# Spreading layer 0 unevenly over the chunks of a state-space scan

## Chip, cores and metric

The kernel runs on one core of a Trainium2 chip. The metric is device time in microseconds (us), from the launch to the end of the core's work; lower is better. Besides the timed runs there is one profiled execution, from which every duration below is taken.

## What is computed

Thirty-two images of 128 channels and 56 x 56 pixels, all float32, go through four layers. Each layer first normalises its input over groups of four channels, and adds its result to the input:

- Layer 0: a 128 x 128 mix of the channels, whose weights depend on the image, and then three depthwise 3 x 3 convolutions of the result with dilations 1, 3 and 5, each through SiLU and added up.
- Layer 1: a fixed cubic spline of each value.
- Layer 2: a linear attention with eight heads, then a depthwise 3 x 3 convolution.
- Layer 3: a Mamba block. Its core is a recurrence over the 3136 pixels of an image, for 256 inner channels with 16 states each.

```python
# layer 0, inside reference(); _gn is the group norm
y = jnp.einsum('boi,bihw->bohw', agg_w, x) + agg_b[:, :, None, None]
for dil in (1, 3, 5):
    c = conv(y, ds_weight, rhs_dilation=(dil, dil), feature_group_count=C)
    out = out + jax.nn.silu(c + ds_bias[None, :, None, None])
...
# layer 3, per token
h = dA_t * h + dBu_t
y = jnp.einsum('bdn,bn->bd', h, C_t)
```

## The kernel before

**Tiling.** An image lies in SBUF as 128 partitions (channels) by 3136 columns, and is worked on in seven chunks of 448 columns (`NCH` = 7). The recurrence of layer 3 treats one chunk in 16 steps (`STEPS`); a step holds two of the 32 pairs of states and channel halves. So an image has 112 steps. In each step VectorE (DVE) multiplies `du` by the rows `pb` (one 128 x 896 multiply, written to `h`) and runs two 448-column scans over `h`; ScalarE (ACT) makes the two decay factors `da`; GpSimd (POOL) multiplies `h` by the rows `cb` into `hc`; TensorE (PE) makes the rows `pb` and `cb`, once in two steps, and adds up `hc` into `y`. Once in a chunk `ssm_inputs` prepares the next chunk on all engines.

**Three images at once.** While the scan of image b runs through its 112 steps, layers 1 and 2 of image b+1 (`until_scan`, called `rest`) and layer 0 of image b+2 (`first_layer`, called `layer0`) are worked on beside it. The function `images` (L1196) lists all this. The steady loop holds six images a pass, runs five passes, and is followed by the last two images; for those no layer 0 is left. A prologue does layer 0 of two images and layers 1 and 2 of one.

**What paces the work beside the scan.** `first_layer` and `until_scan` are Python generators. Each piece of work that they record ends with `yield` of a number, a rough weight. `Pieces.step(i)` takes pieces until the weight taken reaches the share due at step i. For `layer0` the share grows evenly: there are 108 steps (six chunks of 16, and 12 of the seventh), and its total weight is 90. At step 12 of the seventh chunk `layer0.finish()` takes what is left. `rest` is spread over the first 92 steps. The weight of `layer0` is made up of these parts (`dynamic_conv`, L668): statistics of the seven chunks 7, the group's 3, the mixing weights 6, the mixing of one chunk 1 (`aggregate`, seven times), some 4 around them, and 63 for the **depthwise convolutions**, 21 of them at 3 each.

A depthwise convolution of layer 0 is: one load of a stack of shifted rows from DRAM (four DMAs issued on SP), 12 matmuls on PE (`mm<-stack,dsT`; the profile counts each as two records, so 24), a tanh on ACT (`t`), a multiply on DVE (`g`), an addition on POOL (`xt<-xt,g`), and now and then statistics on DVE (`st`). The convolution of layer 2 has the same form (`mm<-stack,wpT`, seven an image), and its output is added by DVE.

**The order on each engine.** The generators do not issue instructions themselves. They record each as a `Work` with the step at which it is taken. `Plan.order` then gives every work a due time, from its step and from what depends on it, and `attempt` lists the works by a model of the engines: of those that are ready on an engine it takes the one that can start first, and of equals the one due first. No work that stands more than 12 steps ahead of the first unfinished one is considered. The resulting lists, one for each engine, are fixed in the program; each engine runs its own in order, and waits at semaphores. So the step at which a piece is taken bounds its place from below, and the plan decides where it ends up.

Of the kernel before, what the change touches and what calls it, by code (L numbers as in the profile page):

```python
# [23 lines left out]
NCH = L // CH  # L24
# [2 lines left out]
UNROLL = 6  # L27

PREP = 17.5
REST = 92  # L30

G = 32
# [36 lines left out]
STEPS = NPAIR * DI  # L69
# [293 lines left out]
def tile_conv_stack(ctx: ExitStack, tc: tile.TileContext, out: bass.AP, x: bass.AP, w: dict):  # L363
# [223 lines left out]
    class Stats:  # L587


        def __init__(self, xt, st=None):  # L590
            self.xt, self.done = xt, 0
            self.st = small.tile([P, NCH, 6], F32, tag="st", name="st") if st is None else st
# [399 lines left out]
    def gate(xn):  # L992

        for db in range(DI):
            ps = psum()
            nc.tensor.matmul(
                ps, wzT[:, db * P : (db + 1) * P], xn[:, DCONV - 1 :], start=True, stop=True
            )
            silu(sz[:, db, :], ps)
            yield 0.8  # L1000
# [138 lines left out]
    def first_layer(src, b):  # L1139

        xt = xts[b % 3]
        for j in range(NCH):
            nc.sync.dma_start(xt[:, j * CH : (j + 1) * CH], src[:, j * CH : (j + 1) * CH])
        yield from dynamic_conv(xt, sts[b % 2])

    def until_scan(b):

        xt = xts[b % 3]
        st = yield from spline(xt, sts[b % 2])
        st = yield from linear_attention(xt, st)  # L1150
        norm = carried[b % 2]
        norm_weights(st, *norm)
        yield 5.0
        layer_norm(xt, xns[b * NCH % 3], 0, norm)
        yield 5.0

    def first_inputs(b):
        return ssm_inputs(xts[b % 3], b * NCH, carried[b % 2])
# [6 lines left out]
    class Pieces:  # L1165


        def __init__(self, gen, total=1.0, steps=1):
            self.gen, self.total, self.steps, self.taken = gen, total, steps, 0.0

        def step(self, i):
            while self.gen is not None and self.taken < self.total * (i + 1) / self.steps:
                self.next()

        def next(self):
# [16 lines left out]
    xv = x.rearrange("b c l -> c b l")  # L1192
# [3 lines left out]
    def images(first, count, ahead):  # L1196

        def image(v, b):  # L1200
            return v[:, ds(first + b, 1), :].squeeze(1)

        scans = {}

        def new_last():
            return small.tile([P, STEPS, 2], F32, tag="last", name="last")

        def at(g, what):

            if 0 <= g < count * NCH * STEPS:  # L1210
                getattr(scans[g // STEPS], what)(g % STEPS)

        plan.start(FIRST)

        for b in range(count):
            xt = xts[b % 3]
            steps = (NCH - 1) * STEPS + READY
            more = b + 1 < count or ahead
            rest = Pieces(until_scan(b + 1) if more else None, totals[1], REST)
            layer0 = Pieces(first_layer(image(xv, b + 2), b + 2) if b + 2 < count or ahead else None, totals[0], steps)  # L1220
            for j in range(NCH):
                k = b * NCH + j
                if k == 0:
                    last = new_last()
                    scans[0] = Scan(xt, image(ov, 0), last, 0)
                    for n in range(AHEAD):
                        at(n, "c_rows")
                    for n in range(2):
                        at(n, "b_rows")
                    at(0, "decay")  # L1230
                following = None
                if j + 1 < NCH:
                    following = ssm_inputs(xt, k + 1, carried[b % 2])
                elif more:
                    following = first_inputs(b + 1)
                following = Pieces(following, PREP, READY)
                gates = Pieces(gate(xns[k % 3]), 1.6, DI)
                for n in range(STEPS):
                    g = k * STEPS + n
                    plan.at(g)  # L1240
                    if n == 0 and j == NCH - 1:
                        rest.finish()
                    if n == READY:

                        following.finish()
                        gates.finish()
                        if j == NCH - 1:
                            layer0.finish()
                        if k + 1 < count * NCH:
                            nb, nj = divmod(k + 1, NCH)  # L1250
                            if nj == 0:
                                last = new_last()
                            scans[k + 1] = Scan(xts[nb % 3], image(ov, nb), last, k + 1)
                    plan.at(g, FIRST)
                    at(g + 2, "b_rows")
                    at(g, "state")
                    at(g + 1, "decay")
                    at(g, "products")
                    at(g + AHEAD, "c_rows")
                    at(g - LAG + 1, "add")  # L1260
                    at(g - LAG, "store")
                    plan.at(g, SECOND)
                    following.step(n)
                    if n >= READY - DI:
                        gates.step(n - READY + DI)
                    plan.at(g)
                    rest.step(j * STEPS + n)
                    if j * STEPS + n > LAG:
                        layer0.step(j * STEPS + n)
        end = count * NCH * STEPS  # L1270
        for g in range(end - LAG + 1, end):
            at(g, "add")
        at(end - 1, "store")
        plan.issue()

    totals = [0.0, 0.0]
# [7 lines left out]
    with tc.For_i(0, B - 2, unroll) as i:  # L1284
        images(i, unroll, True)
    images(B - 2, 2, False)


# [100 lines left out]
```

## Time and profile before

| what | us |
|---|---|
| median of 3 runs (16321.42 to 16344.79) | 16330.96 |
| the profiled execution, launch to end | 16316.11 |
| its span, first to last instruction | 16314.3 |
| start of the first state multiply (end of the prologue) | 436.0 |
| mean time of one of the 30 images of the loop | 499.8 |
| the last two images | 478.7 and 404.6 |

Counting the state multiplies `h<-du,pb` of the trace, 16 to a chunk, splits each image of the loop into its seven chunks. Means over 30 images, in us:

| chunk | first | second | third | fourth | fifth | sixth | seventh |
|---|---|---|---|---|---|---|---|
| length | 63.8 | 70.4 | 70.4 | 73.0 | 70.9 | 80.7 | 70.6 |
| PE busy | 50.1 | 58.7 | 62.9 | 65.2 | 64.8 | 78.1 | 60.4 |
| DVE busy | 60.0 | 63.8 | 62.8 | 63.3 | 66.8 | 67.6 | 62.0 |
| ACT busy | 45.1 | 60.1 | 64.8 | 61.5 | 48.3 | 45.2 | 40.4 |
| POOL busy | 43.3 | 49.1 | 53.4 | 53.7 | 47.0 | 44.2 | 46.3 |

An engine's busy time close to a chunk's length means that the engine has hardly any idle time there. The sum of a row is the engine's work for one image. Since every engine runs its list in order, a chunk is longer than its busiest engine by the waits that no other work covers.

### The profile page before, as it was taken

Reading aid. Unit: us, or ns where it says so; the run is one execution under the profiler, and the core shown is the slowest. Engines: PE = TensorE matmul, PEld = TensorE weight load, DVE = VectorE, ACT = ScalarE, POOL = GpSimd, SP = SyncE. Lnnn points to the kernel's source line nnn. Section 1 sums busy time; section 2 is a strip of 40 time slices with the busy share of each in tenths; the row PEclk is TensorE's granted clock in tenths of the full one; section 3 lists DMA queues with packets and bytes.
Section 4 is the critical chain, followed back from the end, with each engine's and each line's share of the span. In section 5 each row is a group of like instructions: output and inputs, shape, how many; then the busy total and the mean of one; then the engine's idle time right before and its main releaser. Section 6 shows DMA issues by size and latency. Waiting matters only on the chain. (4 is left out here: it accounts for less than half of the span.)

```text
span 16314.3 us, 212520 instructions
## 1 busy us (share of the span) xinstructions
PE 14202.3 (87%) x66400; PEld 4559.9 (28%) x66400; DVE 14306.2 (88%) x17314; ACT 11713.4 (72%) x21127; POOL 10785.0 (66%) x6406
## 2 busy tenths in 40 slices
PE   6888898888898888988888888888888898888887
PEld 2222222222222222222222222222222222222222
DVE  2898988989889898899988888888898898888889
ACT  3777777777677776777776777767777677776675
POOL 2676666666666666667666666666676666766666
PEclk7888998889998898998989988899988899888888
DMA  6344444344443444434444434444344444344421
GB/s 143 93 101 98 98 112 96 89 99 101 106 104 88 100 97 101 109 94 94 101 99 107 102 86 98 99 105 107 91 98 97 100 108 106 85 97 99 101 56 34
DMA packets 986159, 1589.93 MB, mean 97 GB/s; under 512 B 175622, under 2 KB 611209, under 8 KB 984331
## 3 DMA queue, kind: packets, MB, share of 16 engines
q1 hardware_dynamic: 985002, 1576.06, 41.0%
q8 instruction: 538, 8.81, 0.2%
q14 instruction: 619, 5.06, 0.1%
HBM read 785.62 MB, written 173.18 MB: 59 GB/s over the span
## 5 line engine op out<-in xcount | busy, mean ns | idle before, releaser
L338 POOL TENSOR_TENSOR hc<-h,cb 128x896 f32<-128x896 f32 x3584 | 7476.1, 2092 | 4173.5 <-DVE h L338 2178.7
L338 DVE TENSOR_TENSOR_SCAN h<-da,last,h 128x448 f32<-128x448 f32 x6144 | 6772.7, 1135 | 498.2 <-ACT da L338 451.3
L338 ACT ACTIVATE da<-delta,alog 128x448 f32<-128x448 f32 x7168 | 4481.8, 633 | 2635.3 <-DVE h L338 2369.4
L338 PE MATMUL y<-hc,sums 128*64 128x448 f32 x14336 | 3997.9, 638 | 625.6 <-POOL hc L338 617.8
L338 DVE TENSOR_TENSOR h<-du,pb 128x896 f32<-128x896 f32 x3584 | 3788.6, 1072 | 247.5 <-POOL hc L338 118.2
L338 PE MATMUL mm<-stack,dsT 96*32 96x448 f32 (+1 forms) x16128 | 1890.8, 575 | 59.4 <-DMA stack<-padded 16.8
L338 ACT ACTIVATE hats<-stack,bia,scl 128x448 f32<-128x448 f32 x2688 | 1887.6, 754 | 33.9 <-DVE bia L338 31.7
L338 PE MATMUL mm<-xn,winT 128*128 128x448 f32 x3584 | 1703.8, 590 | 39.8 <-ACT cb L338 13.5
L338 PEld LDWEIGHTS y<-hc,sums 128*64 128x64 f32 x14336 | 807.6, 147 | 2412.9 <-POOL hc L338 1436.9
L338 PE MATMUL mm<-hats,wspl 128*32 128x448 f32 x12544 | 1386.1, 563 | 33.3 <-ACT hats L338 30.4
L338 PE MATMUL pb<-dbl,sel 64*128 64x448 f32 x1792 | 918.3, 512 | 421.2 <-DVE h L338 364.3
L338 ACT ACTIVATE hats<-hats,one 128x1344 f32<-128x1344 f32 x896 | 1261.5, 1408 | 0.1
L338 ACT COPY cb<-mm 128x448 f32<-128x448 f32 x1792 | 940.3, 527 | 379.4 <-POOL hc L338 184.0
L338 PE MATMUL mm<-dbl,sel 64*128 64x448 f32 x1792 | 892.3, 502 | 363.5 <-DVE sz L338 63.7
L338 ACT ACTIVATE t<-mm 128x448 f32<-128x448 f32 x1568 | 829.2, 534 | 484.6 <-PE mm L338 480.3
L338 POOL TENSOR_TENSOR xt<-xt,g 128x448 f32<-128x448 f32 x672 | 767.5, 1142 | 524.1 <-DVE g L338 491.1
L338 DVE TENSOR_TENSOR_SCAN h<-da,h 128x448 f32<-128x448 f32 x1024 | 1054.1, 1070 | 28.3 <-ACT da L338 26.3
L338 PEld LDWEIGHTS mm<-xn,winT 128*128 128x128 f32 x3584 | 631.8, 197 | 986.0 <-issue 805.1
L338 DVE SCALAR_TENSOR_TENSOR g<-t,mm 128x448 f32<-128x448 f32 x672 | 407.7, 607 | 443.7 <-ACT t L338 392.8
L338 PEld LDWEIGHTS mm<-stack,dsT 96*32 96x32 f32 (+1 forms) x16128 | 445.2, 112 | 1156.3 <-issue 899.9
L338 PEld LDWEIGHTS mm<-dbl,sel 64*128 64x128 f32 x1792 | 351.2, 198 | 1453.5 <-issue 420.0
L338 PEld LDWEIGHTS pb<-dbl,sel 64*128 64x128 f32 x1792 | 358.6, 200 | 1419.1 <-issue 791.8
(187 smaller groups left out, 16166.2 us busy)
## 6 DMA issues: line engine op xcount, KB each, us to landing
stack<-padded SPq DMA_DIRECT2D x2688, 264.0 KB
stack<-xt SPq DMA_DIRECT2D x3584, 56.0 KB
delta<-delta SPq DMA_DIRECT2D x1792, 112.0 KB
du<-du SPq DMA_DIRECT2D x1792, 112.0 KB
padded<-yc SPq DMA_DIRECT2D x224, 264.0 KB
padded<-yc SPq DMA_DIRECT2D x256, 231.0 KB
xt<-x_dram SPq DMA_DIRECT2D x224, 224.0 KB
out_dram<-xt SPq DMA_DIRECT2D x224, 224.0 KB
```

The costliest lines, as they stand in the source:

```text
L338: call()
```

## The change

`Pieces` takes a list of paces, one for each chunk of the scan, and adds up the paces of the steps to get the share due at each step. `layer0` is given `PACE`; `rest` and the others keep an even pace. With the paces the 90 units of layer 0 fall on the seven chunks as 18.6, 11.4, 14.3, 14.3, 14.3, 0 and 17.1, where they were 13.3 for each of six chunks and 10 for the seventh.

```diff
+PACE = (1.3, 0.8, 1.0, 1.0, 1.0, 0.0, 1.6)
...
-        def __init__(self, gen, total=1.0, steps=1):
-            self.gen, self.total, self.steps, self.taken = gen, total, steps, 0.0
+        def __init__(self, gen, total=1.0, steps=1, pace=(1.0,) * NCH):
+            self.gen, self.taken = gen, 0.0
+            upto = [0.0]
+            for i in range(steps):
+                upto.append(upto[-1] + pace[i // STEPS])
+            self.upto = [total * u / upto[-1] for u in upto[1:]]
 
         def step(self, i):
-            while self.gen is not None and self.taken < self.total * (i + 1) / self.steps:
+            while self.gen is not None and self.taken < self.upto[min(i, len(self.upto) - 1)]:
                 self.next()
...
-            layer0 = Pieces(first_layer(image(xv, b + 2), b + 2) if b + 2 < count or ahead else None, totals[0], steps)
+            layer0 = Pieces(first_layer(image(xv, b + 2), b + 2) if b + 2 < count or ahead else None, totals[0], steps, PACE)
```

Every instruction of the program stays; only the steps at which those of layer 0 are recorded differ, and with them the lists that the plan makes. The number of instructions on each engine, DMAs included, is the same in both programs.

## The prediction

> **What bounds the kernel now.** I read the page's busy shares first:
>
> ```profile
> span 16314.3 us, 212520 instructions
> PE 14202.3 (87%) x66400; PEld 4559.9 (28%) x66400; DVE 14306.2 (88%) x17314; ACT 11713.4 (72%) x21127; POOL 10785.0 (66%) x6406
> ```
>
> TensorE and VectorE are level, and neither is full: an average over stretches with different limits. So next the windows, over the seven chunks of one image (the third of a pass, a typical one; columns as named in the first line, times in us):
>
> ```profile
> core 0: us, PE busy (x) PEld busy (x) DVE busy (x) ACT busy (x) POOL busy (x), PEclk, DMA share, GB/s
> 7430.30:7497.00 66.70, 51.01 (x161) 17.76 (x162) 60.86 (x84) 45.28 (x83) 43.61 (x25) 0.75 0.25 62
> 7497.00:7564.90 67.90, 56.20 (x238) 17.43 (x236) 62.83 (x81) 59.91 (x107) 48.53 (x30) 0.88 0.27 66
> 7564.90:7635.20 70.30, 62.91 (x337) 19.23 (x338) 63.12 (x74) 65.73 (x116) 54.07 (x34) 0.97 0.47 113
> 7635.20:7707.00 71.80, 64.65 (x349) 19.63 (x351) 62.66 (x74) 60.66 (x110) 53.10 (x33) 0.93 0.39 90
> 7707.00:7777.00 70.00, 63.48 (x329) 24.54 (x322) 66.82 (x83) 48.37 (x91) 47.17 (x30) 0.93 0.47 107
> 7777.00:7858.70 81.70, 78.91 (x430) 23.19 (x432) 67.73 (x79) 45.56 (x91) 44.41 (x25) 0.98 0.60 140
> 7858.70:7924.20 65.50, 55.22 (x248) 18.07 (x240) 60.91 (x72) 40.22 (x65) 45.89 (x29) 0.95 0.50 116
> ```
>
> The sixth chunk stands out: 81.70 us, PE busy for 78.91 of them. In the others DVE is the fullest engine, or ACT in the third (65.73 of 70.30). Then the groups of the sixth chunk, DVE first (after the second bar: idle time before the group, and what ended it):
>
> ```profile
> L338 DVE SCALAR_TENSOR_TENSOR g<-t,mm 128x448 f32<-128x448 f32 x5 | 3.1, 610 | 6.1 <-ACT t L338 6.1
> L338 DVE SCALAR_TENSOR_TENSOR xc<-t,mm 128x448 f32<-128x448 f32 x2 | 1.2, 620 | 3.2 <-ACT t L338 3.2
> L338 DVE SCALAR_TENSOR_TENSOR sz<-t,mm 128x448 f32<-128x448 f32 x3 | 1.8, 609 | 2.4 <-ACT t L338 2.4
> L338 PE MATMUL mm<-stack,dsT 96*32 96x448 f32 (+1 forms) x120 | 13.8, 548 | 0.0
> L338 PE MATMUL mm<-stack,wpT 96*32 96x448 f32 x152 | 15.8, 545 | 0.0
> ```
>
> DVE's idle time there is mostly before three multiplies that need a tanh `t`, 11.7 us; and over the whole span the tanh itself waits for the matmul in front of it (480.3 of its 484.6 us idle, `t<-mm` on the page). Five of the waiting ones are `g`, layer 0's own. So here PE is late, DVE stands in its list before `g`, and the scans behind `g` stand with it. Last, finer windows of the same image: steps 24 to 35, then 80-83, 84-87, 88-91, 92-95 and 96-99:
>
> ```profile
> 7527.90:7580.60 52.70, 44.88 (x202) 13.89 (x206) 46.96 (x53) 46.75 (x83) 37.63 (x23) 0.87 0.37 94
> 7777.00:7795.80 18.80, 18.80 (x69) 5.49 (x68) 15.59 (x18) 11.47 (x24) 9.44 (x6) 0.91 0.34 93
> 7795.80:7819.00 23.20, 22.94 (x118) 7.00 (x120) 16.64 (x19) 10.43 (x23) 8.64 (x6) 1.00 0.53 127
> 7819.00:7839.60 20.60, 19.73 (x126) 5.85 (x130) 17.97 (x23) 12.10 (x22) 11.60 (x6) 1.00 0.60 143
> 7839.60:7858.70 19.10, 17.44 (x128) 4.85 (x120) 17.54 (x22) 11.57 (x24) 14.73 (x8) 1.00 0.93 199
> 7858.70:7876.20 17.50, 14.94 (x79) 5.05 (x73) 17.46 (x25) 6.84 (x12) 9.08 (x7) 1.00 0.86 196
> ```
>
> PE is saturated from 80 to 91. The five last rows add to 99.2 us, with PE busy 93.85 and DVE 85.20. The first row, where work will be added, has idle time on every engine.
>
> **What the Trainium skill says.** "Perfetto Trace Analysis", Identifying the Most-Contended Engine: the busy share of matmuls does not measure how far TensorE is from its peak. The trace agrees that it is no peak figure (weight loads are busy for only 23.19 of the 81.70 us), so I rest the claim that PE binds on DVE's waits, not on the share. The same page, Optimization Strategy: where the most-contended engine changes over time, interleaving the regimes may help; here the regime changes in the sixth chunk, and the change takes work out of the stretch where PE binds. "TensorE: Matmul & The Clock Gate", What's actually happening: the PE clock is halved after idle windows and released by activity; in the trace the granted clock is 0.75 in the first chunk and 1.00 from step 84, so the same matmul can cost more where it is moved. The same page, Architectural detail: ACT and DVE are strict queues; the `g` waits above show it.
>
> **The change part by part.** The steps in the code do not tell where the instructions land, so I compared the built orders. On PE's list, counted by the `pb` rows (one in two steps), the 21 depthwise convolutions of layer 0 end in these steps (first image of a pass before, second after; the others differ by a step or two):
> before 36 38 42 46 50 54 58 62 64 70 74 78 82 84 88 92 96 98 102 102 108;
> after 28 32 38 44 48 50 54 56 60 64 68 72 74 78 82 84 96 100 102 110 112.
>
> So between 36 and 87 there are 14 in both; two move to steps 28 to 35, and one to step 112, the first of the next image's scan (in five of six images; at the end of a pass it comes at 110). Between 88 and 99 the list holds 48 `dsT` matmuls before and 16 after, on the mean of four images: 32 / 12 = 2.7 convolutions fewer. Layer 2's seven convolutions stay, and end at 94 instead of 96. Instruction counts do not change, so nothing is won but waits.
>
> 1. *Taken out of 88-99.* One convolution is 24 records; 120 of them took 13.8 us, so 2.75 us each. 2.7 x 2.75 = 7.4 us. Matmuls overlap: the chunk's PE rows add to 91.0 us for 78.91 busy, so 0.87 of it counts: **6.4 us off the path**, once an image. DVE does not bind instead: it goes from 85.20 to about 83.5 (2.7 `g` at 0.61 us), PE from 93.85 to 87.5.
> 2. *The one put to step 112.* The next image's steps 0-3 took 13.90 us with PE busy 13.56. Cost between 0 (its `g` fits in a wait) and 2.75 x 0.87 = 2.4. PE has no room, so I take 2.0; in 5 of 6 images, **1.7 us**.
> 3. *The two put to 28-35.* 4.8 us of PE into a stretch (24-35) with 7.8 us of PE idle, 5.7 of DVE, 6.0 of ACT. Cost between 0 and 4.8; a quarter, **1.2 us**, since most of it fits and some comes at the wrong moment, at a clock of 0.87.
> 4. *The rest.* The mixing matmuls (7.8 us an image) start at 22 instead of 28, where PE has room; the x loads and the padded stores move on SP with them. Nothing taken: DMA is busy 41% of the span, DVE's waits for DMAs are under 1 us an image. In exchange the stack loads of layer 2 meet fewer of layer 0 in the sixth chunk, where the DMA share reaches 0.93; nothing taken either.
> 5. *The spline of the next image* needs layer 0's last piece. Its biases `bia` stand at steps 11-12 of DVE's list before and 11 after; nothing.
>
> Sum: -6.4 + 1.7 + 1.2 = -3.5 us an image. Prologue and last two images (436.0 and 883.3 us) hold no paced layer 0 and stay. 30 x 3.5 = 105: the profiled 16316 becomes 16211. The median of the runs is 15 above the profiled time, so **16226**, -0.64%. Lists change everywhere a little, and placement has luck in it: the fourth chunk takes some 71.6 us in five images of a pass and 79.7 in one. That is 1.3 us an image, or 40 us; with the bounds of 2 and 3 the forecast's own range is 16130 to 16300.
>
> **Rivals.**
>
> - *No change* (16331): the gain of 1 is smaller, because in 88-99 the chain head matmul, `kx`, store, stack load, convolution of layer 2 sets the pace and not the volume of PE. For: ACT `kx` waits for PE. Against: PE had at most 1 us idle in 80-91.
> - *More than forecast* (16031): with PE relieved, steps 80-99 fall to DVE's pace. In the fifth chunk DVE is busy 0.955 of the time; 83.5 / 0.955 = 87.4 in place of 99.2, -11.8, less about 1.8 for points 2 and 3: -10 x 30 = -300. Against: layer 2's heads and convolutions remain there on PE, at 87.5.
> - *Slower* (16451): the moved convolutions land in lists in which every engine waits for the other, so each costs its PE time and its DVE time one after the other: 2.4 on PE, 0.61 for `g`, and 0.66 for its mean wait (443.7 / 672 on the page), 3.7 us. 2.83 of them cost 10.4, net +4.0 x 30 = +120. It decides once more than 6.4 of the 10.4 falls on the path, 62%. For: the second and third chunks have ACT and DVE at 85 to 93%, and the seventh ends with the convolutions at 110 and 112 in front of the next image. Against: the 5.7 us of DVE idle time in 24-35.
> - *The plan ignores the paces*, since it may fill in anything up to 12 steps ahead. Against: the orders above; the gap from 84 to 96 is there.
>
> **How the numbers follow.** About 0.2% (33 us) is what a measurement of this kernel can tell from no change. Chances: forecast 0.48, no change 0.16, more 0.12, slower 0.24. Nearly all of the forecast and all of "more" are faster by over 0.2%: 0.60; same 0.15; slower 0.25. The range 16060 to 16440 takes in the forecast's own range, no change, and half of each outer case, which leaves some 0.17 out.
>
> **What would show it.** In the profile after: the sixth chunk at about 75 us and no longer alone, no `dsT` in its second half, `g` waits there near 1 us instead of 6; the first chunk some 2 us longer, the second 1. The forecast is wrong if the sixth chunk stays above 79 (the heads' chain binds), or if it shortens and the first, second and seventh chunks together grow by more than it lost.

## The result, and the profile after

The changed kernel takes 16391.1 us (median of 7 runs, 16377.94 to 16397.6); the kernel before, beside it, 16330.96 (16314.49 to 16355.59). The ratio is 1.0033, with a 95% interval of 1.0021 to 1.0045: slower by a third of a per cent. The prediction was 16226. The profiled execution's span is 16389.0 us, 74.7 more than before.

Mean lengths of the chunks over the 30 images of the loop, in us, with the time in which DVE works and the remainder:

| chunk | first | second | third | fourth | fifth | sixth | seventh | image |
|---|---|---|---|---|---|---|---|---|
| before | 63.8 | 70.4 | 70.4 | 73.0 | 70.9 | 80.7 | 70.6 | 499.8 |
| after | 64.5 | 73.7 | 72.5 | 77.1 | 72.0 | 73.6 | 68.8 | 502.4 |
| difference | +0.7 | +3.3 | +2.1 | +4.1 | +1.1 | -7.1 | -1.8 | +2.5 |
| of it, DVE busy | +2.2 | +1.0 | -0.6 | +2.7 | -0.4 | -2.8 | -0.7 | +1.4 |
| of it, DVE idle | -1.5 | +2.3 | +2.7 | +1.4 | +1.5 | -4.3 | -1.1 | +1.1 |

30 x 2.5 is 76 us, about the whole difference of the spans. The sixth chunk lost 7.1 us, and the four chunks from the second to the fifth took 10.6 us back. The gain does not end with the sixth chunk: over steps 80 to 99, the stretch of the prediction's finer windows, the mean of the 30 images went from 100.1 to 89.5 us, and over steps 88 to 99 alone from 58.8 to 49.5.

DVE's busy time grew by 1.4 us an image, although its instructions are the same. Most of that lies in a few tiny instructions, such as `dm<-mv,mg`, a subtraction on one column. The groups before and after:

```profile
L338 DVE TENSOR_TENSOR dm<-mv,mg 128x1 f32<-128x1 f32 x128 | 35.9, 281 | 0.7
L339 DVE TENSOR_TENSOR dm<-mv,mg 128x1 f32<-128x1 f32 x128 | 75.4, 589 | 0.1
```

Of the 128, 17 took longer than 0.4 us before and 62 after. Every one of these 79 began while POOL's multiply `hc<-h,cb` was running and ended 13 to 21 ns after it did. So part of what the page counts as work of DVE looks like a wait for POOL, and it too depends on how the lists meet. That POOL's multiply is the cause was not tested.

The means also hide that the same chunk differs between the six images of a pass, which have the same work. In the fourth chunk two of the six take 73.0 us on average and the other four 78.7 to 79.5; before, one took 79.7 and the others some 71.6. In the fifth chunk the first image takes 85.9 us and the others 68.0 to 73.9; before, all took 69.9 to 73.5. The whole +1.1 us of the fifth chunk comes from that first image; the other five together became shorter.

The busy shares, from the page of the changed kernel, show none of this:

```profile
span 16389.0 us, 212620 instructions
PE 14177.3 (87%) x66400; PEld 4501.4 (27%) x66400; DVE 14348.0 (88%) x17314; ACT 11737.7 (72%) x21127; POOL 10794.5 (66%) x6406
```

The windows of the same image as before (the third of the third pass), its seven chunks:

```profile
core 0: us, PE busy (x) PEld busy (x) DVE busy (x) ACT busy (x) POOL busy (x), PEclk, DMA share, GB/s
7469.00:7533.57 64.57, 49.61 (x179) 16.11 (x179) 63.16 (x82) 44.98 (x83) 46.62 (x27) 0.82 0.33 84
7533.57:7606.72 73.15, 63.30 (x278) 19.52 (x282) 64.88 (x84) 62.06 (x112) 51.22 (x32) 0.87 0.31 79
7606.72:7679.98 73.26, 65.36 (x324) 19.56 (x318) 62.96 (x72) 64.06 (x114) 51.80 (x32) 0.87 0.37 87
7679.98:7752.90 72.92, 64.89 (x334) 19.21 (x334) 63.73 (x74) 60.82 (x110) 54.80 (x34) 0.92 0.51 118
7752.90:7826.83 73.93, 71.22 (x375) 25.49 (x374) 68.10 (x85) 50.11 (x95) 48.31 (x31) 0.93 0.43 99
7826.83:7898.69 71.86, 70.02 (x370) 20.89 (x368) 64.07 (x75) 43.48 (x87) 40.97 (x23) 1.00 0.56 138
7898.69:7966.61 67.92, 57.13 (x218) 17.16 (x217) 60.76 (x73) 40.22 (x66) 42.51 (x26) 0.83 0.41 92
```

The sixth chunk fell from 81.70 to 71.86 here, and no longer stands out. The second grew from 67.90 to 73.15: PE does 7.1 us more in it, DVE 2.1, and the chunk is longer by 5.3. No engine is full in it.

Three groups of DVE in the sixth chunk, the ones that waited for a tanh before:

```profile
L339 DVE SCALAR_TENSOR_TENSOR sz<-t,mm 128x448 f32<-128x448 f32 x3 | 1.8, 608 | 0.0
L339 DVE SCALAR_TENSOR_TENSOR xc<-t,mm 128x448 f32<-128x448 f32 x2 | 1.2, 622 | 3.2 <-ACT t L339 3.2
L339 DVE SCALAR_TENSOR_TENSOR g<-t,mm 128x448 f32<-128x448 f32 x2 | 1.2, 608 | 3.1 <-ACT t L339 3.1
```

And PE's convolution matmuls in its second half, steps 88 to 95 alone:

```profile
L339 PE MATMUL mm<-stack,wpT 96*32 96x448 f32 x120 | 12.4, 545 | 0.2 <-DVE sz L339 0.2
```

There is no `dsT` group in steps 88 to 95 any more; layer 2's convolutions (`wpT`) have them to themselves. DVE's wait before `g` went from 6.1 us to 3.1, that before `sz` from 2.4 to none, and that before `xc` stayed at 3.2. (On the mean of the 30 images the wait before `g` in this chunk went from 5.9 to 4.1.) The finer windows, steps 80-83, 84-87, 88-91, 92-95 and 96-99:

```profile
7826.83:7842.27 15.44, 15.44 (x64) 4.73 (x63) 14.65 (x18) 10.33 (x23) 9.45 (x6) 1.00 0.41 115
7842.27:7865.09 22.82, 22.55 (x118) 6.81 (x118) 16.53 (x20) 10.61 (x23) 8.25 (x6) 1.00 0.53 128
7865.09:7881.76 16.67, 16.10 (x94) 4.92 (x98) 16.60 (x21) 11.17 (x21) 9.64 (x5) 1.00 0.51 127
7881.76:7898.69 16.93, 15.93 (x102) 4.42 (x94) 16.29 (x21) 11.38 (x22) 13.63 (x8) 1.00 0.80 183
7898.69:7914.57 15.88, 14.38 (x79) 4.29 (x78) 15.88 (x25) 6.12 (x12) 8.38 (x5) 1.00 0.70 157
```

They add to 87.7 us, where before they added to 99.2. In steps 88 to 91 DVE is now the fuller engine (16.60 of 16.67, PE 16.10), where PE was before (19.73 of 20.60, DVE 17.97). In the two windows behind it DVE was the fuller one already, and these too are shorter, by 2.2 and 1.6 us.

### The profile page after: what moved, and what is told of

It reads as the page before. It is cut to its first block, busy times and chain, and to the rows that moved or that the text cites. A ratio compares the mean times of both kernels' runs of the same rounds, so it can differ in the third digit from the quotient of the medians.

```text
span 16389.0 us, 212620 instructions
## 1 busy us (share of the span) xinstructions
PE 14177.3 (87%) x66400; PEld 4501.4 (27%) x66400; DVE 14348.0 (88%) x17314; ACT 11737.7 (72%) x21127; POOL 10794.5 (66%) x6406
## 5 line engine op out<-in xcount | busy, mean ns | idle before, releaser
L339 PE MATMUL mm<-stack,dsT 96*32 96x448 f32 (+1 forms) x16128 | 2085.2, 626 | 91.0 <-DVE cube L339 27.9
L339 PE MATMUL mm<-xn,winT 128*128 128x448 f32 x3584 | 1633.1, 571 | 38.8 <-DVE g L339 22.7
```

Of the source, the lines that this page charges most:

```text
L339: call()
```

## The experiments

Eighteen kernels were run. Each is timed beside the kernel before; the ratio is to that, with its 95% interval, and the chunks are means over the 30 images of the loop.

| run | ratio | interval | first | second | third | fourth | fifth | sixth | seventh |
|---|---|---|---|---|---|---|---|---|---|
| e2_late | 1.0007 | 0.9999-1.0016 | 63.8 | 71.2 | 72.0 | 73.2 | 78.0 | 73.2 | 68.9 |
| e1_rate | 1.0044 | 1.0030-1.0058 | 64.6 | 72.3 | 75.0 | 72.1 | 76.7 | 73.0 | 68.5 |
| e5_front | 1.0183 | 1.0169-1.0197 | 61.0 | 74.4 | 73.4 | 72.9 | 79.7 | 78.8 | 69.8 |
| j1_jitter | 0.9953 | 0.9939-0.9966 | 62.2 | 72.6 | 70.3 | 71.1 | 77.4 | 76.7 | 67.2 |
| warm_before | 1.0032 | 1.0021-1.0043 | 63.9 | 70.8 | 70.9 | 72.7 | 74.9 | 79.4 | 70.9 |
| warm_changed | 1.0175 | 1.0160-1.0189 | 64.3 | 74.2 | 72.2 | 77.2 | 77.9 | 74.2 | 69.0 |
| warm_late | 1.0034 | 1.0022-1.0046 | 63.6 | 71.0 | 71.6 | 72.8 | 82.9 | 73.1 | 68.8 |
| x_pe | 1.0024 | 1.0013-1.0036 | 64.1 | 73.8 | 71.6 | 77.6 | 72.5 | 73.6 | 68.7 |
| x_chain | 1.0016 | 1.0007-1.0024 | 64.2 | 73.8 | 71.6 | 77.2 | 72.5 | 73.7 | 68.6 |
| jitter_changed | 1.0079 | 1.0065-1.0093 | 64.1 | 73.9 | 75.4 | 73.2 | 76.1 | 73.4 | 68.9 |
| jitter_even2 | 1.0054 | 1.0041-1.0068 | 65.0 | 70.1 | 70.4 | 72.0 | 74.4 | 81.6 | 70.7 |
| jitter_changed2 | 1.0218 | 1.0204-1.0232 | 64.2 | 75.0 | 80.3 | 70.0 | 80.2 | 73.8 | 68.4 |
| sp_before | 1.0231 | 1.0217-1.0245 | 63.6 | 70.9 | 70.9 | 75.2 | 72.0 | 89.3 | 70.9 |
| sp_changed | 1.0356 | 1.0342-1.0370 | 64.1 | 73.7 | 77.3 | 78.6 | 71.9 | 82.5 | 70.8 |
| sp_late | 1.0352 | 1.0338-1.0367 | 63.5 | 71.2 | 72.1 | 76.4 | 78.1 | 81.8 | 74.9 |
| sp_jitter | 1.0406 | 1.0389-1.0423 | 64.2 | 74.6 | 80.2 | 75.0 | 75.3 | 82.0 | 70.7 |
| spline_changed | 1.0053 | 1.0039-1.0066 | 64.4 | 73.7 | 70.3 | 78.6 | 72.9 | 73.7 | 69.0 |
| spline_jitter | 1.0059 | 1.0046-1.0073 | 64.9 | 73.6 | 71.4 | 74.6 | 75.6 | 73.3 | 69.3 |

### Other paces: is it the work that was moved forward?

Only the line `PACE` differs from the changed kernel's.

```diff
-PACE = (1.3, 0.8, 1.0, 1.0, 1.0, 0.0, 1.6)
+PACE = (1.0, 1.0, 1.0, 1.0, 1.0, 0.0, 2.33)      # e2_late
+PACE = (1.45, 1.0, 1.0, 1.0, 1.0, 0.0, 1.73)     # e1_rate
+PACE = (1.45, 1.0, 1.0, 1.0, 1.0, 1.0, 0.4)      # e5_front
+PACE = (1.0, 1.0, 1.0, 1.0, 1.0, 1.0, 1.1)       # j1_jitter
```

> Paces (1,1,1,1,1,0,2.33): the sixth chunk's share goes to the seventh alone. On TensorE's list the first 14 depthwise convolutions end at the same steps as before (36 to 84), none from 85 to 95, seven from 96 to 112. Theory V (volume: a depthwise convolution costs some 3 to 5 us in the second to fifth chunks, as much as it gives back in the sixth): second to fifth chunks as before (284.7 us together, within 1), sixth 74, seventh and first together longer by 4 to 7; ratio to before 0.994 to 1.000. Theory L (luck: any new list meets other stalls): second to fifth chunks off by several us although nothing moves into them.

> Paces (1.45,1,1,1,1,0,1.73): sixth chunk empty as in the changed kernel, two convolutions put early as there, but after them the same pace as before in the second to fifth chunks. Theory V: two more convolutions in the second to fifth chunks still cost some 10 us an image together, so about 1.003 as the changed kernel. A third theory D (density: the 7% faster pace of the changed kernel in the third to fifth chunks makes the stalls) has these chunks back at the lengths of before, 1 to 3 us for the second chunk, and a ratio near 0.994.

> Paces (1.45,1,1,1,1,1,0.4): the early front of e1_rate alone; the sixth chunk keeps its share, the seventh gives two convolutions to the second. Theory V: second to fifth chunks longer by about 10 us together, sixth as before at 80 to 81, seventh shorter by 3 to 6: ratio 1.007 to 1.014. Theory L: no rule. Theory D: 0.998 to 1.004.

> Control: paces (1,1,1,1,1,1,1.1), so nearly even; convolutions stand at the same steps as before or two later. Theory V and D: within 0.1% of before, each chunk within 1 us. Theory L: the total moves by 0.2 to 0.5% either way, and single chunks by 2 us and more, with nothing moved between them.

e2_late leaves the first 14 convolutions where the kernel before has them (they end in the same steps, 36 to 84), and puts the other seven into steps 96 to 112. Its sixth chunk is 7.5 us shorter, like the changed kernel's. But its second to fifth chunks, into which nothing was moved, take 294.4 us where before took 284.7: the gain is given back where no volume was added. The traces bear out that nothing was moved in: these four chunks hold 288 records of `dsT` matmuls an image in both kernels, that is 12 convolutions; in the changed kernel they hold 336. So theory V, which had these chunks unchanged, is refuted, and "the moved convolutions cost it" cannot be the whole. In total e2_late is the same as the kernel before (the interval takes in 1). e1_rate, which fills the first chunk and keeps the next four even, is no better, so theory D fails too; e5_front, which keeps the sixth chunk filled and thins the seventh, is the worst of the four, and slower than theories V and D had it.

j1_jitter was meant as the control: it is nearly even, and differs from the kernel before only by the seventh chunk's pace, 1.1 instead of 1: 10.9 of layer 0's 90 units fall there instead of 10. It is faster than before by 0.47% (0.34 to 0.61), and the fastest kernel of this study: 16244.27 us beside 16317.55. Its sixth chunk is 4.0 us shorter, its fifth 6.5 longer. A change of paces by some per cent is thus worth as much as the change that was made, and here in the other direction. Theories V and D had this kernel within 0.1% of before; only theory L allowed for it.

### The two early convolutions by themselves

x_pe issues, for layer 0's first two convolutions of an image, only the 4 matmuls of the first row of taps and leaves out the 8 of the other two. x_chain leaves out their tanh, `g` and the addition to `xt`. In both the planner still sees the work, so that every list is otherwise as in the changed kernel.

```diff
+            plan.mute = cut and i > 0          # x_pe: rows of taps, cut = first two convolutions
...
+            plan.mute = i < 2                  # x_chain
             silu(g[:], ps)
             nc.gpsimd.tensor_add(xt[:, cols], xt[:, cols], g[:])
+            plan.mute = False
```

> The changed kernel; of the first two depthwise convolutions of layer 0 of each image, those at steps 28 to 35, only 4 of the 12 matmuls are issued (left out: the middle and lower row of taps). The order of all else on every engine is unchanged, since what is left out is still planned and priced. 3.7 us of TensorE work an image less. If these two cost what their TensorE time is (theory V on TensorE), the second and third chunks fall from 146.2 us together by 2.5 to 3.7; if TensorE has room there, by under 1. Ratio to before 0.996 or 1.003.

> The changed kernel; for the same two convolutions the tanh on ACT, the multiply g on DVE and the addition on POOL are not issued (left out: their result). Order of all else unchanged. 1.2 us of DVE, 1.1 of ACT and 2.3 of POOL work an image less, and the wait of g for its tanh. If the early convolutions cost through DVE's list, the second and third chunks fall by 2.5 to 6 us together; if through TensorE, by under 1.5.

The groups by line of the changed kernel and of x_pe show what was taken out (count, then busy us and mean ns):

```profile
L339 PE MATMUL mm<-stack,dsT 96*32 96x448 f32 (+1 forms) x16128 | 2085.2, 626 | 91.0 <-DVE cube L339 27.9 <-DMA stack<-padded 26.3 <-DVE sz L339 12.5
```
```profile
L340 PE MATMUL mm<-stack,dsT 96*32 96x448 f32 (+1 forms) x15104 | 1936.3, 616 | 91.6 <-DVE cube L340 27.4 <-DMA stack<-onesd 21.7 <-DMA stack<-padded 18.2
```

1024 records and 149 us of them are gone, 4.7 us for each of the 32 images. Second and third chunk together go from 146.3 us to 145.4, 0.8 less, and the image from 502.4 to 502.0. x_chain takes 0.9 to 1.0 off them, to 145.3, and has an image of 501.5. The expectation of x_pe had less than 1 us if TensorE has room there, and that is what came; that of x_chain had 2.5 to 6 us if the convolutions cost through DVE's list, and that did not come. Before, the two chunks took 140.8. So what was left out of the two convolutions accounts for some 1.8 us of the 5.5 that these two chunks lost, if the two parts add; most of the rest is there without them. It is not all of the two: a third of their matmuls and their loads were still issued. The ratios of both kernels overlap with the changed kernel's 1.0021 to 1.0045, so the sizes rest on one profiled execution of each.

### TensorE's clock in the fifth chunk

In the fifth chunk kernels differ by up to 9 us. Over 180 images of six kernels (before, changed and the four above) its length goes with the time in which the trace shows TensorE at half clock in it (correlation 0.87; about 65.5 us plus half of that time). Two windows of one image of e2_late, its fifth and sixth chunk:

```profile
7717.71:7795.13 77.42, 70.78 (x338) 28.17 (x339) 67.55 (x84) 51.65 (x98) 45.76 (x30) 0.85 0.43 98
7795.13:7868.88 73.75, 71.91 (x377) 21.27 (x374) 65.46 (x76) 43.75 (x86) 43.24 (x24) 1.00 0.55 134
```

The granted clock is 0.85 in the fifth, 0.93 in the same chunk before, though PE is busy for 91% of it in both. The Trainium skill, "TensorE: Matmul & The Clock Gate", What's actually happening, has the clock halved after idle windows and released by activity. The traces agree that the clock is either full or half, and that it changes by windows: of the 384 half-clock stretches in the kernel before, all but the cut-off last one are multiples of 3.4 us long. In 28 of its 30 images, and in 23 of e2_late's, such a stretch begins within 6 us of the first of layer 2's narrow matmuls (two columns each, steps 77 and 78); in the others it had begun earlier. If the lack of activity decides here, more activity should help: the warm kernels add four 128x448 matmuls, whose result nobody reads, between these narrow ones. The planner does not see them; all lists are else unchanged.

```diff
         for h in range(HEADS):
...
+                if h % 2:
+                    plan.group.calls.append(warm(pbt))
```

> e2_late with four extra 128 x 448 matmuls an image, whose results nobody reads, put among the 16 two-column matmuls of layer 2 (mm<-bv and mm<-nm); they are not priced, so the order of all other instructions on every engine is that of e2_late. Theory C (clock: the fifth chunk is as long as TensorE's half-clock time there makes it, 65.5 us plus half of that time; e2_late has 25.4 us of it where before has 12.6): half-clock time in the fifth chunk falls to 10 to 18 us, and the chunk from 78.0 to 71 to 75 us, although 3 us of TensorE work is added; total faster than e2_late by 0.6 to 1.2%, ratio to before 0.989 to 0.995. Theory V or L without the clock: the chunk grows by up to 3 us, ratio 1.001 to 1.007.

> The changed kernel with the same four unpriced matmuls. Theory C: the fifth chunk of the first image of a pass (85.9 us with 29.8 us at half clock) falls to 70 to 78; the other five (68 us with 10 to 14) change by -1 to +3; ratio to before 0.999 to 1.004. The fourth chunk keeps its 77 us, since its stall is another. Without the clock: all six images 2 to 3 us longer, ratio 1.007 to 1.010.

> Control: the kernel before with the same four unpriced matmuls. Theory C: little to win (12.6 us at half clock in the fifth chunk), so -2 to +2 us an image, ratio 0.996 to 1.004. Without the clock: +3 us an image, ratio 1.005 or more.

This failed. Half-clock time in the fifth chunk went from 25.4 to 26.5 us an image (warm_late), 12.6 to 10.6 (warm_before) and 14.7 to 17.2 (warm_changed), and the chunk became longer by 4.9, 4.0 and 5.9. The sums hide that the start did move: in warm_before no half-clock stretch begins within 6 us of the first narrow matmul in any of the 30 images; in 12 one begins some 10 us after it, in 15 none follows in the chunk, and in 3 it had begun earlier. In warm_late it had begun earlier in 10 images, and 129 of the 240 added records ran at half clock themselves. The added matmuls take 6.1, 4.6 and 5.9 us of PE an image, where the expectation had 3: 80% to all of it lands on the path, more than either theory had. What can be carried from it is that PE's time at steps 77 and 78 is uncovered. What causes the half clock there is not settled, and that it is cause and not companion of the longer chunk isn't shown.

### How much is luck of the lists

Three more kernels, in which a pace of the kernel before or of the changed one is off by a few per cent (j1_jitter above was the first of this kind):

```diff
+PACE = (1.0, 1.0, 1.0, 1.0, 1.03, 1.0, 1.0)      # jitter_even2
-PACE = (1.3, 0.8, 1.0, 1.0, 1.0, 0.0, 1.6)
+PACE = (1.3, 0.8, 1.0, 1.0, 1.03, 0.0, 1.6)      # jitter_changed
+PACE = (1.25, 0.85, 1.0, 1.0, 1.0, 0.0, 1.6)     # jitter_changed2
```

> Control of the changed kernel: the pace of the fifth chunk 1.03 instead of 1.0, all else as there; the depthwise convolutions stand at the same steps or two later. If placement alone makes half a per cent, as j1_jitter showed for even paces, this moves by 0.2 to 0.6% from the changed kernel's 1.0033, either way, and single chunks (the fourth and fifth above all) by 2 us or more. If not, it stays within 0.1% of 1.0033.

> A third even draw: pace of the fifth chunk 1.03, all others 1.0. By what two even kernels (1.000, 0.9953) and two of the change's kind (1.0033, 1.0079) show, placement scatters by some 0.3 to 0.5%; this should lie between 0.993 and 1.003. If it lies above 1.003, the even kernels and the changed ones cannot be told apart, and the change's loss is placement alone.

> A third draw of the change's kind: paces (1.25, 0.85, 1, 1, 1, 0, 1.6), first depthwise convolution at 32 instead of 28 or 30. Expected between 1.002 and 1.010 if emptying the sixth chunk costs in itself, at or below 1.000 if the loss is placement alone. Second and third chunks together 146 to 149 us (140.8 before), sixth 73 to 74.

jitter_changed did what its expectation had for placement: the fourth chunk is 3.9 us shorter, the fifth 4.1 longer, and the time 0.5% longer than the changed kernel's. The other two missed their ranges. jitter_even2 lies above 1.003, where its expectation said that the two kinds cannot be told apart. jitter_changed2 lies above both of its branches; its second and third chunks take 155.2 us, where 146 to 149 were expected.

Even paces give 1, 0.9953 and 1.0054; the changed ones 1.0033, 1.0079 and 1.0218. Within each group the spread is at least 1%, that is 165 us and more. The groups overlap, and three of each are too few to tell whether an emptied sixth chunk is by itself worth less than nothing (means 1.0002 and 1.0110). None of the five kernels with an emptied sixth chunk (with e2_late and e1_rate) was faster than the kernel before. What all five share is its 73 to 74 us, and 49.5 us for steps 88 to 99 (58.8 before); where they differ is mainly the second to fifth chunk, from 294.4 to 305.5 us (284.7 before).

One meeting of the lists, in the timeline of the changed kernel (start, duration, engine, instruction; in brackets the idle time before it and what ended it). It is the fourth chunk of the tenth image:

```profile
5223.66 3.22 PE L339 MATMUL mm<-stack,dsT 97*32 97x448 f32 x16
...
5226.65 1.81 PE L339 MATMUL mm<-hats,wspl 128*32 128x448 f32 x16
...
5228.29 0.93 PE L339 MATMUL mm<-stack,dsT 96*32 96x448 f32 x8
...
5229.04 1.68 PE L339 MATMUL mm<-hats,wspl 128*32 128x448 f32 x16
...
5230.04 0.62 DVE L339 TENSOR_TENSOR xt<-xt,mm 128x448 f32<-128x448 f32 x1 [4.46 <-PE mm L339]
```

DVE's next entry is the spline's addition. Its matmuls (`wspl`) stand on PE behind 16, and around 8 more, of a layer-0 convolution, which DVE does not wait for at that moment. DVE stands for 4.46 us, and with it the scan. In the image before, PE starts the same stretch 2.6 us ahead of DVE's multiply `h<-du,pb` (4718.33 and 4720.96 us) instead of 1.95 us behind it (5223.66 and 5221.71), and the wait is 0.48 us: PE's pieces are the same, only the lists are laid past each other by 4.6 us. Over the fourth chunk this wait rose from 1.75 us an image to 3.31, and those of `cube` for POOL's `xt` from 0.34 to 1.43.

### The waits for du: many meetings, or one cause?

The largest single new wait was that of `h<-du,pb` at step 48 for the DMA that spreads `du` over the partitions. The view of tile `du`, for DVE, gives what ended the idle time before it (us, times), in the changed kernel and in jitter_changed:

```profile
  PE pb L339: 85.5, 105
  POOL hc L339: 73.9, 108
  DMA du<-du: 70.2, 32
```
```profile
  DMA du<-du: 206.0, 48
  PE pb L339: 92.7, 99
```

Before it was 20.8 us. 15.9 us of it stand at the first two steps of the first image, in both of these kernels and before. The rest, nearly all at steps 48 and 49, is 54 us in the changed kernel and 190 in jitter_changed; before, it was 5, and none of it there. The timeline of SP's queue in jitter_changed, around step 48 of an image:

```profile
4667.22 3.07 SPq L339 DMA_DIRECT2D delta<-delta  x5
4670.39 10.56 SPq L339 DMA_DIRECT2D stack<-xt  x16
4681.05 2.48 SPq L339 DMA_DIRECT2D du<-du  x4
4683.58 1.89 SPq L339 DMA_DIRECT2D delta<-delta  x3
4685.57 1.19 SPq L339 DMA_DIRECT2D du<-du  x2
```

The 16 loads of the spline's next chunk take 10.56 us of SP's time, 0.66 each, and `du` stands behind them although the spline needs them only a chunk later.

The first remedy put every `delta` and `du` DMA on SP right behind the last work that it depends on. The lists of the other engines are unchanged. (The expectation speaks of loads of convolution stacks; the 16 loads `stack<-xt` are the spline's.)

```diff
         order, works = self.order(), self.works
+        last, placed = {}, []
+        for i in order:
+            if works[i].soon:
+                placed.insert(placed.index(last[i]) + 1 if i in last else 0, i)
+            else:
+                placed.append(i)
...
                         nc.sync.dma_start(dst[Q * s : Q * s + Q, r, :], src[Q * r : Q * r + Q, db, :])
+                        plan.works[-1].soon = True
```

> The changed kernel; only SP's own list differs: each DMA that spreads delta or du over the partitions for the scan is issued right behind the work it depends on, so that no loads of convolution stacks stand in front of it. Theory Q (the moved stack loads delay du on SP, and this is a main part of what the change loses): DVE's waits of h for the DMA du fall from 70.2 us over the span (20.8 in the kernel before) to under 20, the fourth chunk comes down from 77.1 by 2 us, and the ratio goes from 1.0033 to about 1.000. Theory L (the loss lies in how PE's, DVE's and POOL's re-laid lists meet, and du is one of many): the waits go as in Q, but the ratio stays within 1.001 to 1.003. Against both: SP waits at the moved DMAs for the engines that write du, the stack loads behind them come later, and the ratio rises above 1.0033.

> jitter_changed with the same change of SP's list, where the waits for du are the largest: 206 us over the span. Theory Q: they fall to under 30, the third chunk comes down from 75.4 by about 4 us, and the ratio from 1.0079 by at least 0.008 to 1.000 or below. Theory L: the waits go, but something else on the same steps is late next, and the ratio falls by less than half of that, to 1.004 or more. Against both: as in sp_changed.

> e2_late with the same change of SP's list; its waits for du are 105 us over the span. Theory Q: they fall to under 25 and the ratio from 1.0007 by 0.004 to about 0.997. Theory L: the ratio falls by less than half of that, to 0.999 or more.

> The kernel before with the same change of SP's list: the control. Its waits for du are only 20.8 us over the span, so both theories give a ratio of 0.999 to 1.001. If it comes out below 0.998, the change of SP's list is worth something by itself, which would then have to be taken off the gains of the other three.

All four are slower by 2 to 3.5%, the control too: the third outcome. In each the sixth chunk grew by about the same, 8.6 (before), 8.9, 8.6 and 8.6 us. SP's queue in the sixth chunk of the changed kernel, then of sp_changed, same image:

```profile
7883.03 0.34 SPq L339 DMA_DIRECT2D padded<-yc  x1
7884.73 3.04 SPq L339 DMA_DIRECT2D delta<-delta  x5
7887.87 1.48 SPq L339 DMA_DIRECT2D stack<-padded  x3
```
```profile
8125.47 1.25 SPq L349 DMA_DIRECT2D stack<-padded  x3
8134.12 5.86 SPq L349 DMA_DIRECT2D delta<-delta  x8
8140.09 0.53 SPq L349 DMA_DIRECT2D padded<-yc  x1
8140.72 4.96 SPq L349 DMA_DIRECT2D du<-du  x8
8145.78 3.10 SPq L349 DMA_DIRECT2D stack<-padded  x6
```

In the first, layer 2's store `padded<-yc` goes out 1.3 us after step 92 begins (7881.76), ahead of `delta`. In the second, SP issues nothing from 8126.7 to 8134.1, when `delta` can go, and the store stands behind it: 8.9 us after step 92 begins (8131.15), with the stack's load behind `du`. The group of layer 2's additions on DVE in that chunk, before and after this edit:

```profile
L339 DVE SCALAR_TENSOR_TENSOR xt<-mm,wpb,xt 128x448 f32<-128x448 f32 x7 | 4.7, 670 | 0.0
```
```profile
L349 DVE SCALAR_TENSOR_TENSOR xt<-mm,wpb,xt 128x448 f32<-128x448 f32 x7 | 4.7, 673 | 8.9 <-PE mm L349 8.9
```

One badly placed block on SP costs 8.9 us an image in that chunk, more than the sixth chunk won by being emptied. The images as a whole grew by 12.8 to 17.9 us; what cost the rest was not followed up. The edit also made the waits for `du` longer instead of shorter (197.0 us over the span in sp_changed, 95.6 in sp_before), so it tells nothing of what it was made for.

The second remedy moves only the spline's loads, and only those that stand directly in front of `delta` and `du`: to right behind them, eight times in six images.

```diff
+        for i in [i for i in order if works[i].sort == "spline"]:
+            k, behind = order.index(i), None
+            while k + 1 < len(order) and order[k + 1] not in works[i].next:
+                k += 1
...
+            if behind is not None:
+                order.remove(i)
+                order.insert(order.index(behind) + 1, i)
```

> The changed kernel; on SP's list alone, eight times in six images, the 16 loads stack<-xt of the spline's next chunk are moved from in front of a chunk's delta and du DMAs to right behind them. Nothing is put in front of layer 2's stores and loads, as sp_changed did. Theory Q (du behind the spline's loads is a main part of the loss): DVE's waits of h for du fall from 70.2 us over the span to under 20, the spline's additions, prepared one chunk ahead, lose nothing, the fourth chunk comes down from 77.1 by about 2 us and the ratio from 1.0033 to about 1.000. Theory L (many meetings of the lists, of which du is one): the waits for du go, but the ratio stays within 1.001 to 1.004, since the spline's matmuls come later and its additions (xt<-xt,mm) wait instead.

> jitter_changed with the same move, there also eight times in six images. Theory Q: the waits for du fall from 206 us to under 40, the third chunk comes down from 75.4 by about 4 us and the ratio from 1.0079 by 0.008 or more. Theory L: the ratio falls by less than half of that.

The same view of tile `du`, in spline_changed and in spline_jitter:

```profile
  PE pb L353: 87.9, 104
  POOL hc L353: 74.8, 114
  DMA du<-du: 15.9, 2
```
```profile
  PE pb L353: 178.0, 134
...
  DMA du<-du: 15.9, 2
```

Now the waits were hit: of 32 and 48 two are left in each, those at the start of the first image. The third chunk, which ends with the wait at step 48, gets shorter by 2.2 and by 4.0 us, to 70.3 and 71.4 (for spline_changed theory Q had named the fourth). But the time does not follow. In spline_changed the fourth chunk grows by 1.5 us and the fifth by 0.9, the image takes 502.7 instead of 502.4, and the ratio is 1.0053 where the changed kernel had 1.0033 (the intervals overlap). In spline_jitter the fourth grows by 1.4, the waits for `pb` from PE rise from 92.7 to 178.0 us, and the ratio falls from 1.0079 to 1.0059: 0.2% for 190 us of waits, which are 1.2% of the time. Theory L stands, with a ratio in spline_changed a little above its 1.001 to 1.004, and not by its own reason, since the spline's additions wait no longer than before in the fourth chunk (3.3 us an image in the changed kernel and in spline_changed). What waits instead is `g` for its tanh in the fourth chunk of spline_changed (0 to 1.2 us an image) and `kb` for PE in the fifth (1.1 to 1.8); in the fourth chunk of spline_jitter, `pb` (0.1 to 2.8) and the multiply `sz<-sz,y` for `y` (0.1 to 2.6), both from PE. With one late transfer mended, the next engine in line is late instead.

## Why the prediction was wrong

**What failed is item 4, "The rest ... Nothing taken", with the sentence that lists "change everywhere a little" and that this be worth 40 us.** It priced the moved pieces and took the re-laid lists around them to be neutral. Against the -3.5 us an image of the sum, the image took +2.5. Steps 80 to 99 gave more than forecast, 10.6 us; the steps outside them cost 13.2, where items 2 and 3 had 2.9. Most of it, 10.6, is the second to fifth chunks, and of this the two early convolutions by themselves cost some 1.8. The remaining 9 us are what the re-laid lists cost, since nothing but the lists differs between the programs. That the volume moved is not needed for such a loss is shown by e2_late (+9.7 there without moving anything in), and its size by the jitter kernels (changes of 0.5 to 2% by paces off by a few per cent). The 40 us were one image's luck in one chunk; the runs show at least 1% between kernels that hardly differ. A forecast of -0.64% was inside that, so its direction had no support; the chance of 0.60 for faster was too high.

Point by point:

- *Item 1*, 6.4 us out of steps 88-99: they lost 9.3, in all five kernels with an empty sixth chunk. The mechanism was right, and the size too small by a third. The trace has 53 records of `dsT` fewer there, 2.2 convolutions instead of 2.7, so each was worth more than its PE time; DVE's idle time in the sixth chunk fell by 4.3 us with it. The waits for `g` did not fall to 1 us, but to 3.1 in the image shown.
- *Item 2*, 1.7 us for the convolution at step 112: steps 0 to 3 of the next image became 1.4 longer, and the first chunk 0.7. The seventh chunk gained 1.8, but only by its first four steps (-3.5), which belong to item 1; its other twelve, for which nothing was said, became 1.7 longer.
- *Item 3*, 1.2 us for the two early convolutions: 0.8 for two thirds of PE's part and 0.9 to 1.0 for the chain behind it. About right, a little low.
- *Item 4 on DMAs*: "DVE's waits for DMAs are under 1 us an image" was read before the change and held to stay so. The waits for `du` became 1.8 us an image of the loop (0.1 before). Mended, they returned nothing, so this is an instance of the failed step and not the cause.
- *The fifth item*, the spline's biases: nothing of it shows in the first chunk.
- *Rivals.* "Slower" had the direction, with 16451, but by a mechanism which x_pe and x_chain speak against: the two early convolutions cost some 1.8 us together, not 3.7 each. "No change" is refuted by steps 88 to 99. "More than forecast" had the right stretch and nearly the right size, -11.8 us for steps 80 to 99 against the measured -10.6; it failed by the same step as the forecast, since it too took nothing for the lists elsewhere. (It also took 1.8 us for items 2 and 3, which add to 2.9.) The two signs of failure that were named were a sixth chunk above 79, and a growth of the first, second and seventh chunks beyond the gain; those three grew by 2.2 together. More than half of the loss came in the third to fifth, which no sign covered.
- *The range*, 16060 to 16440, holds the 16391, which is luck: the errors of -10.6 instead of -6.4 and of +13.2 instead of +2.9 partly cancel.

What stays open: whether an emptied sixth chunk is on average a loss, a gain or neither in this kernel; and how far the clock is part of the loss. In the second to fifth chunks together TensorE spent 8.6 us an image more at half clock in the changed kernel than before (7.3 of it in the third), and 21.7 more in e2_late. At half of that time, as in the fifth chunk above, an estimate gives some 4 of the 10.6 us and about all of e2_late's 9.7. No run separates this from the waits that go with it, and why the half clock comes and goes isn't shown.

## What to carry to other kernels

Where a planner lays out every engine's list, a change of due times is a new draw of all lists: before forecasting a gain below a per cent, measure the spread of the time over a few trivial variations of the input to the planner, and put that into the range. A wait that is removed is worth what the next-late engine leaves of it; with five queues that wait for each other, that was nothing in one kernel here and, by the ratios, about a sixth in another. And where such a spread exists, try several draws and keep the best: paces of 1 with 1.1 in the last chunk took 0.5% less than the kernel before and 0.8% less than the changed one, more than the considered change.

## What the runs showed of the hardware

- Issuing the 16 small spline loads occupies SP's queue for 10.0 us and more (10.56 in the image shown, 0.66 each), and eight `delta` or `du` DMAs for 5.0 to 5.9. Whatever is queued behind them is issued that much later. SP is no engine of the busy shares, and the order of its list alone moved the time by 2.3% (sp_before) to 3.4% (sp_late, 1.0352 against 1.0007 without the edit).
- TensorE was granted 0.93 and 0.85 of its clock in two fifth chunks in both of which it was busy for 91%. Stretches at half clock were multiples of 3.4 us long, and in 28 of 30 images of the kernel before one began within 6 us of the first matmul of two columns. Four added matmuls of 128x448 moved that start (in none of 30 images within 6 us in warm_before), but took more time than they saved (the chunk became 4.0 us longer).
- A DVE instruction on one column, `dm<-mv,mg`, took 0.13 us at the least and up to 1.56. All 79 that took more than 0.4 us in the kernels before and after began during POOL's multiply of 128x896 and ended 13 to 21 ns after it. The trace counts this as DVE's busy time.
